# First layer of a graph network: row norms in two chains of four blocks, weight sums held behind the scaled rows, the last four blocks turned together

## The chip, the cores and the metric

The kernel runs on one core of a Trainium2 chip. The metric is the device time of one execution in microseconds (us); the median of several runs is given. In the traces PE is TensorE (matrix products), PEld its loads of stationary operands, DVE is VectorE, ACT ScalarE, POOL GpSimd, and SP the engine that issues most of the transfers.

## The reference

The input x has 1024 rows of 512 values (float32). Rows are normalised and clipped at zero, normalised by column, and passed through a graph convolution with 16384 edges and a loop at each node. Four layers of attention and a gated feed-forward part follow, then a second graph convolution, and x is added. In short:

```python
h = jnp.maximum(_layernorm(x), 0.0); x_in = h
h = gcn((h - mu) * rsqrt(var + EPS) * bn_w + bn_b, src, dst, gcn_in_w, gcn_in_b)
for i in range(4):
    a = attn(ln(h, ln2_w[i], ln2_b[i]), cond, Wq[i], Wk[i], Wv[i], Wo[i])  # 16 groups of 64 rows, 8 heads of 64
    h = h + a
    u = ln(h, ln3_w[i], ln3_b[i]) @ geglu_w[i] + geglu_b[i]
    val, gate = jnp.split(u, 2, axis=-1)
    h = h + (val * gelu(gate)) @ ffo_w[i] + ffo_b[i]
h = gcn(h, src, dst, gcn_out_w, gcn_out_b)
return x + h + x_in
```

Each group attends to 256 condition rows: `cond` has 16 x 256 x 512 values. The kernel treats two groups, 128 rows, as one block; there are eight blocks.

## The kernel before

Rows are held as eight blocks of 128 partitions, `h[0]` to `h[7]`, slices of one tile `hall`. Products are float32. Large products are split in two by two halves and done with seven half products instead of eight (Strassen's scheme in Winograd's form); `sums_of_a` and `sums_of_b` make the sums of halves that this needs, mostly on GpSimd, in four operations for each operand: `weight_sums` for a weight, `sum_cond` for a condition block, `sum_first` for the turned rows of one pair of blocks (`nb` and `nb + 4`).

`seven` does the seven half products for the keys and the values. It holds three banks of PSUM, `b`, `c`, `d` (and `a`). Product 5 goes to `b`, 6 to `c`, 4 to `d`; VectorE makes `u2` from `b` (L713), `u3` from `c` (L716) and writes `c22` from `d` (L718). Then product 3 starts anew in `c` and product 2 in `d`, and VectorE writes `c21` (L723) and `c12` (L725). In the trace both `u2` and `u3` are called `u_k` or `u_v`, and the banks `pb_k`, `pc_k`, `pd_k` or `pb_v` and so on. Products 0 and 1 of the keys of blocks 0 and 1 and of the values of block 0 are done early (`begin`).

The stretch that the change touches lies between the first graph convolution and the queries of the first layer. `aggregate` multiplies the edge counts with the rows, block by block, 16 matmuls a block (blocks 0 and 1 together), and calls `into_h_and_norm`: `into_h` (L672) evicts the block into `h[d]`. After blocks 1 and 3, `ready_first` normalises a pair: `moments` takes `bn_stats` and `bn_aggr` of each block (L155, L156), then `rsqrt`, a chain of 11 small operations (L134, L136, and three times L139, L141, L143) on one column for each block, then `scaled` writes the scaled rows `xn` (L164). `turn_first` transposes scaled rows on TensorE (`tr_ln`, four transposes a block) and writes them with weight and bias into `lnT`, half on ScalarE (L690) and half on VectorE (L688). Behind the aggregates stand, on TensorE: the keys of block 0, the turning of blocks 0 to 3, the values of block 0, the turning of blocks 4 and 5, the keys of block 1, the turning of blocks 6 and 7, and the queries (`qa` and on).

The kernel is written with tile pools; a scheduler orders the instructions of each engine by its own estimate of times, and each engine then runs its list in that order. `tc.issue_after(ins)` keeps what is written under it behind an instruction in the order of issue. `waiting_for(ins, engine)` adds a true wait: the instructions of that engine that are written under it wait until `ins` is done.

Of the kernel before, what the change touches and what calls it, by code (L numbers as in the profile page):

```python
# [8 lines left out]
F32 = mybir.dt.float32  # L9
# [5 lines left out]
OP = mybir.AluOpType  # L15
AX = mybir.AxisListType

P = 128
EPS = 1e-5
# [4 lines left out]
def gnn_kernel(  # L24
# [26 lines left out]
    nc = tc.nc  # L51
# [23 lines left out]
    small = ctx.enter_context(tc.tile_pool(name="small", bufs=4))  # L75
# [5 lines left out]
    @contextmanager  # L81
    def waiting_for(ins, engine):

        traced = nc.cur_bb.bb.instructions
        n = len(traced)
        yield
        for i in traced[n:]:
            if i.engine == engine:
                tc.add_manual_dep(i, ins.ins.name, mybir.DependencyInfo(
                    mybir.DependencyClass.Sync, mybir.DependencyReason.DATA))  # L90
# [33 lines left out]
    def rsqrt(var, name, eps=0.0):  # L124


        k = var.shape[1]

        def t(n, dtype=F32):
            return small.tile([P, k], dtype, tag=f"rs_{n}{k}", name=f"{n}_{name}",  # L130
                              bufs=4 if k == 1 else 2)

        v = t("v")
        rsqrt.first = nc.vector.tensor_scalar(v, var, float(eps), None, OP.add)  # L134
        y = t("y")
        nc.vector.tensor_scalar(y.bitcast(I32), v.bitcast(I32), -0.5, RSQRT_SEED, OP.mult, OP.add)  # L136
        for i in range(3):
            a = t("a")
            nc.vector.scalar_tensor_tensor(a, y, -0.5, v, OP.mult, OP.mult)  # L139
            b = t("b")  # L140
            nc.vector.tensor_tensor(b, a, y, OP.mult)  # L141
            y2 = t("y")
            nc.vector.scalar_tensor_tensor(y2, b, 1.5, y, OP.add, OP.mult)  # L143
            y = y2
        return y

    def moments(xts, name, kept=None):

        n = len(xts)
        mv = kept  # L150
        if mv is None:
            mv = small.tile([P, 2 * n], F32, tag=f"mv{n}", name=f"mv_{name}", bufs=2)
        for i, xt in enumerate(xts):
            st = small.tile([P, 6], F32, tag="st", name=f"st_{name}_{i}")
            nc.vector.bn_stats(st, xt)  # L155
            nc.vector.bn_aggr(mv[:, 2 * i:2 * i + 2], st)  # L156
        return mv, rsqrt(mv.rearrange("p (n c) -> p n c", c=2)[:, :, 1], name, EPS)

    def scaled(xts, mv, rstd, name, to=None):

        xns = []
        for i, xt in enumerate(xts):
            xn = to[i] if to else t512(f"xn_{name}_{i}")
            nc.vector.tensor_scalar(xn, xt, mv[:, 2 * i:2 * i + 1], rstd[:, i:i + 1],  # L164
                                    OP.subtract, OP.mult)
            xns.append(xn)
        return xns

# [28 lines left out]
    h = [hall[:, nb, :] for nb in range(NB)]  # L197
# [18 lines left out]
    def halves_of(t):  # L216
        return t.rearrange("p (a b) -> p a b", a=2)
# [21 lines left out]
    def sum_cond(g, t):  # L239

        b = [t[i][:, j, :] for i in range(4) for j in range(2)]
        sums_of_b(nc.gpsimd, b[0], b[2], b[1], b[3], b[4], b[5], b[6])
        unsaved.append((g, t))
# [34 lines left out]
    conds = {}  # L278
# [18 lines left out]
    def blocks_out(t):  # L297

        return [t[d][:, :, b * M:(b + 1) * M] for d in range(2) for b in range(2)]

    def of_k(w, right):
        return lambda i, to, start: multiply(
            to, w[i], right[i], [(c * P, (c + 1) * P, 0, M) for c in range(2)], start)
# [28 lines left out]
    raw_wk = load_w(Wk[0], "wk_0")  # L332
    fetch_cond(1)
    w_in = load_w(gcn_in_w, "w_in")
    raw_wv = load_w(Wv[0], "wv_0")
# [71 lines left out]
    with tc.issue_after(load_pe.ins), tc.issue_after(load_act.ins):  # L407
        turned = [turn_cond(0, (0, 0))]
# [4 lines left out]
    with tc.issue_after(outside_last.ins):  # L413
        mean, root = moments(xb, "x", x_mean.rearrange("p a b -> p (a b)"))
# [217 lines left out]
    root = rsqrt(pdeg[:, :NB], "deg")  # L632
# [59 lines left out]
    def weight_sums(w, name):  # L692

        s = slots_of(2, name)
        blk = blocks_of_w(w)
        s1, s2, s4 = (halves_of(s[i // 2][:, i % 2, :]) for i in range(3))
        sums_of_a(nc.gpsimd, *blk, s1, s2, s4)
        return [blk[0], blk[1], s4, blk[3], s1, s2, blk[2]]

    def seven(name, product, c11, c12, c21, c22, s1=None):  # L700

        b, c, d = (bank(f"{n}_{name}") for n in ("pb", "pc", "pd"))
        begun = s1 is not None
        if not begun:
            a = bank(f"pa_{name}")
            product(0, a, True)
            s1 = acc_tile(f"s1_{name}")
            nc.scalar.copy(s1, a)  # L710
        product(5, b, True)
        u2 = acc_tile(f"u2_{name}")
        nc.vector.tensor_tensor(u2, b, s1, OP.add)  # L713
        product(6, c, True)
        u3 = acc_tile(f"u3_{name}")
        nc.vector.tensor_tensor(u3, c, u2, OP.add)  # L716
        product(4, d, True)
        nc.vector.tensor_tensor(c22, halves_of(d), halves_of(u3), OP.add)  # L718
        if not begun:
            product(1, a, False)  # L720
            nc.scalar.copy(c11, halves_of(a))
        product(3, c, False)
        nc.vector.tensor_tensor(c21, halves_of(c), halves_of(u2), OP.add)  # L723
        product(2, d, False)
        return nc.vector.tensor_tensor(c12, halves_of(d), halves_of(u2), OP.add)  # L725

    def keys(l, g, wk, begun=None):
        kT, s1 = begun or (slots_of(2, f"kT_{l}_{g}"), None)
        return kT, seven(f"k_{l}_{g}", of_k(wk, conds[l, g]), *blocks_out(kT), s1)

    def values(l, g, wv, begun=None):
        v, s1 = begun or (slots_of(2, f"v_{l}_{g}"), None)
        v11, v21, v12, v22 = blocks_out(v)
        seven(f"v_{l}_{g}", of_v(wv, conds.pop((l, g))), v11, v12, v21, v22, s1)
        return v
# [267 lines left out]
    def sum_first(t, nb):  # L1003

        c0 = nb % 4 * P
        of = [lnT[i][k][:, :, c0:c0 + P] for k in range(2) for i in range(2)]
        sums_of_b(t, *of, *(x[:, :, c0:c0 + P] for x in lnS))

    xns = {}

    def into_h_and_norm(d, pa):
        into_h(d, pa)
        if d in (1, 3):
            ready_first(0, [d - 1, d])

    def ready_first(l, blocks):
        for i in range(0, len(blocks), 2):
            pair = blocks[i:i + 2]
            xns.update({nb: h[nb] for nb in pair} if l == L else norm(pair, f"ln2_{l}_{pair[0]}"))

    def turn_first(l, blocks):

        for nb in blocks:
            xn, c0 = xns.pop(nb), nb % 4 * P
            if l < L:
                turn(xn, lnT[nb // 4], c0, LN2W + l * KC, LN2B + l * KC, f"ln2_{l}_{nb}")
            else:
                pt = transposed(xn, f"hT_{nb}")
                for k in range(2):
                    nc.scalar.copy(lnT[nb // 4][k][:, :, c0:c0 + P],  # L1030
                                   four(pt)[:, 2 * k:2 * k + 2, :])
# [6 lines left out]
    def load_rest(l):  # L1038
        return (load_w(Wq[l], f"wq_{l}"), load_w(Wo[l], f"wo_{l}"),
                load_row(ffo_b, l * D, f"ffb_{l}"))  # L1040
# [13 lines left out]
            nc.gpsimd.dma_start(again[d].bitcast(F32R).rearrange("p a b -> p (a b)"), c_dram[d])  # L1054
        return w, bias

    projections = (weight_sums(raw_wk, "wks_0"), weight_sums(raw_wv, "wvs_0"), *load_rest(0))
    sum_cond(1, turned[1])
    with tc.issue_after(load_w.last.ins):
        for d in range(NB):  # L1060
            nc.sync.dma_start(c_dram[d], C[d].rearrange("p a b -> p (a b)"))
    for l in range(L):

        wk, wv, wq, wo, ffb = projections
        if l:
            wq = weight_sums(wq, f"wqs_{l}")
            lnS = slots_of(3, f"ln2S_{l}")
            sum_first(nc.gpsimd, 0)
            sum_first(nc.gpsimd, 1)
            kv_next = kv(l, 0, wk, wv, lambda: ready_first(l, left_to_turn[2:]))  # L1070
            turn_first(l, left_to_turn)
            next_cond(l, 1)
            sum_first(nc.vector, 2)
            sum_first(nc.vector, 3)
        else:
            lnS = slots_of(3, f"ln2S_{l}")
            kT, last_key = keys(0, 0, wk, begun["k0"])
            with tc.issue_after(last_key.ins):
                ready_first(0, [4, 5])
                turn_first(0, [0, 1, 2, 3])  # L1080
                kv_next = kT, values(0, 0, wv, begun["v0"])
                ready_first(0, [6, 7])
            turn_first(0, [4, 5])
            wq = weight_sums(wq, "wqs_0")
            sum_first(nc.gpsimd, 0)
            sum_first(nc.gpsimd, 1)
            kT_1, _ = keys(0, 1, wk, begun["k1"])
            turn_first(0, [6, 7])
            sum_first(nc.vector, 2)
            sum_first(nc.vector, 3)  # L1090
        qT = queries(l, wq)

        ln3T = [slots_of(2, f"ln3T_{l}_{i}") for i in range(2)]
# [188 lines left out]
```

## Time and profile before

| | |
|---|---|
| median of 3 runs | 2551.42 us (2549.64 to 2553.30) |
| profiled execution | 2551.04 us, of which the profile's span is 2549.3 us |
| mean granted clock of TensorE | 0.999 |
| TensorE busy | 2520.1 us (99%) |
| VectorE busy | 1398.5 us (55%) |
| ScalarE busy, GpSimd busy | 550.9 us, 554.5 us (22% each) |
| from the first key product to the first query product | 119.89 to 156.36 us |

Busy time counts instructions that run; matmuls follow each other in a pipeline, so the end of one is modelled and lies past the start of the next. "Idle before" is the time in which an engine had nothing running, and the name behind the arrow is what it waited for. The granted clock is a share of full speed. Times in timelines count from the start of the span.

### The profile page before, as it was taken

The page shows a single profiled execution, that of the slowest core. Times are in us where ns is not written, and L with a number is a line of the kernel's source. Part 1 is how long each engine was busy: PE and PEld are TensorE (multiplying, and loading weights), DVE is VectorE, ACT ScalarE, POOL GpSimd, SP SyncE. Part 2 cuts the span into 40 slices and gives each one's busy share as a digit, 9 for nine tenths or more (in the row PEclk, how much of TensorE's full clock was granted, in tenths as well). Part 3 has the DMA queues.
Part 4 walks back from the last instruction along what each step waited for, and adds up shares of the span by engine and source line. Part 5 has one row for each costly group of instructions (what it writes and reads, how often), then busy time and mean ns, then how long its engine had stood idle before and what let it go on. Part 6 is the DMA issues. An engine that isn't in the chain of part 4 may idle for free. (4 is left out here: it accounts for less than half of the span.)

```text
span 2549.3 us, 31825 instructions
## 1 busy us (share of the span) xinstructions
PE 2520.1 (99%) x12320; PEld 1744.8 (68%) x12320; DVE 1398.5 (55%) x3060; ACT 550.9 (22%) x1294; POOL 554.5 (22%) x423
## 2 busy tenths in 40 slices
PE   8999999999999999999999999999999999999999
PEld 5668886665578887555587888556676888566565
DVE  9765555544564555644475555644474555554561
ACT  7322222111122222111122222211112222211111
POOL 0401123422300002333310002233310002331410
PEclk9999999999999999999999999999999999999999
DMA  6402223110211111110212211110111112111020
GB/s 177 150 9 92 91 74 121 33 50 12 84 49 67 59 55 58 55 49 17 80 44 75 71 55 58 54 47 20 58 66 59 58 59 67 54 33 62 13 87 34
DMA packets 67133, 156.77 MB, mean 61 GB/s; under 512 B 5576, under 2 KB 5904, under 8 KB 66976
## 3 DMA queue, kind: packets, MB, share of 16 engines
q1 hardware_dynamic: 64880, 149.25, 17.8%
q0 software_dynamic: 1376, 4.30, 0.5%
q8 instruction: 101, 1.65, 0.3%
q10 hardware_dynamic: 720, 1.11, 0.1%
q14 instruction: 56, 0.46, 0.1%
HBM read 133.66 MB, written 20.97 MB: 61 GB/s over the span
## 5 line engine op out<-in xcount | busy, mean ns | idle before, releaser
L293 PE MATMUL ga<-ln3T,wval 128*128 128x512 f32 x512 | 233.9, 593 | 0.0
L1101 POOL TENSOR_TENSOR hall<-hall,ffb 128x512 f32<-128x512 f32 x28 | 35.6, 1271 | 782.4 <-DVE xn_ln L164 782.4
L867 ACT ACTIVATE g<-g,gcols 128x512 f32<-128x512 f32 x128 | 92.3, 721 | 431.8 <-DVE g L880 367.2
L293 PEld LDWEIGHTS ga<-ln3T,wval 128*128 128x128 f32 x512 | 96.0, 190 | 109.9 <-issue 109.1
L765 ACT ACTIVATE pr<-sc,nmax 128x256 f32<-128x256 f32 x256 | 118.2, 474 | 170.7 <-DVE nmax L760 170.5
L941 POOL TENSOR_TENSOR hall<-fu,hall 128x512 f32<-128x512 f32 x24 | 30.5, 1270 | 467.9 <-DVE fu L940 467.9
L293 PE MATMUL pc_k<-ct,wk 128*128 128x256 f32 x512 | 122.7, 383 | 5.0 <-DVE u_k L716 5.0
L293 PE MATMUL fa<-wff,fT 128*128 128x256 f32 x512 | 121.6, 379 | 0.0
L293 PE MATMUL gc<-ln3S,wgate 128*128 128x512 f32 x256 | 120.4, 592 | 1.1 <-DVE gu L877 1.1
L293 PE MATMUL pa_v<-wv,ct 128*128 128x256 f32 x512 | 121.1, 379 | 0.0
L293 PE MATMUL pd_k<-ct,wks 128*128 128x256 f32 x512 | 121.0, 379 | 0.0
L293 PE MATMUL pc_v<-wv,ct 128*128 128x256 f32 x512 | 121.0, 379 | 0.0
L293 PE MATMUL pd_v<-wvs,ct 128*128 128x256 f32 x512 | 120.9, 379 | 0.0
L293 PE MATMUL gb<-ln3S,ges 128*128 128x512 f32 x256 | 120.6, 593 | 0.0
L293 PE MATMUL gd<-ln3T,ges 128*128 128x512 f32 x256 | 120.5, 593 | 0.0
L293 PE MATMUL gd<-ln3S,ges 128*128 128x512 f32 x256 | 120.3, 592 | 0.0
L293 PE MATMUL gc<-ln3T,wgate 128*128 128x512 f32 x256 | 120.3, 592 | 0.0
L816 PE MATMUL pw<-wo,oT 128*128 128x512 f32 x256 | 118.0, 604 | 0.0
L293 PE MATMUL pa_k<-ct,wk 128*128 128x256 f32 x480 | 113.7, 380 | 0.0
L293 PEld LDWEIGHTS fa<-wff,fT 128*128 128x128 f32 x512 | 97.3, 190 | 21.8 <-issue 9.6
L293 PEld LDWEIGHTS pc_k<-ct,wk 128*128 128x128 f32 x512 | 98.2, 192 | 19.3 <-issue 2.9
L293 PEld LDWEIGHTS pa_k<-ct,wk 128*128 128x128 f32 x480 | 90.7, 190 | 23.5 <-issue 11.9
(288 smaller groups left out, 4719.8 us busy)
## 6 DMA issues: line engine op xcount, KB each, us to landing
ct<-cond_dram SPq DMA_DIRECT2D x72, 512.0 KB, 4.4
wval<-in_L_gnn_geglu_w_dram SPq DMA_DIRECT2D x32, 512.0 KB, 4.4
wgate<-in_L_gnn_geglu_w_dram SPq DMA_DIRECT2D x32, 512.0 KB, 4.6
wff<-in_L_gnn_ffo_w_dram SPq DMA_DIRECT2D x32, 512.0 KB, 4.3
cond_dram<-ct SPq DMA_DIRECT2D x24, 512.0 KB, 3.6
cond<-in_L_gnn_cond_dram SPq DMA_DIRECT2D x32, 256.0 KB, 4.6
ct<-cond_dram SPq DMA_DIRECT2D x24, 256.0 KB, 4.4
wk<-in_L_gnn_Wk_dram SPq DMA_DIRECT2D x8, 512.0 KB, 5.5
```

The lines of the kernel that those rows point to most:

```text
L293: nc.tensor.matmul(at, left[:, k, l0:l1], right[:, k, r0:r1], start=start and n == 0 and k == 0, stop=n == len(cols_of) - 1 and k == 1, sk ...
L765: nc.scalar.activation(pr3[:, a, :], ps3[:, a, :], AF.Exp, bias=nmax[:, a:a + 1], accum_out=tot[:, a:a + 1])
L816: nc.tensor.matmul(pw, oT[:, c * P:(c + 1) * P], wo[c // 2][:, c % 2, :], start=(c == 0), stop=(c == HP - 1))
L867: nc.scalar.activation(pre, pre, AF.Gelu, bias=gcols[:, cg:cg + 1])
L941: t.tensor_tensor(h21, halves_of(u2), h21, OP.add)
L1101: t.tensor_tensor(h[nb], h[nb], ffb, OP.add)
```

## The change

The norms of the first layer's first half are no longer taken pair by pair. Each block's moments are taken when the block is evicted, into one of two tiles `mv_first` of four blocks each. After block 3 one `rsqrt` chain on four columns serves blocks 0 to 3, and their four rows are scaled. The second chain, for blocks 4 to 7, is issued behind `c22` of the first keys (`beside` in `seven`), and their rows are scaled behind the last operation of these keys. On GpSimd the sums of the first layer's `Wv` and of condition 1 wait until the first four rows are scaled, and the sums of `Wq` until the last four are. Blocks 4 to 7 are turned together, ahead of the keys of block 1, and VectorE's sums of turned blocks are issued behind these keys.

```diff
@@ -144,25 +144,33 @@
             y = y2
         return y
 
-    def moments(xts, name, kept=None):
-
-        n = len(xts)
-        mv = kept
-        if mv is None:
-            mv = small.tile([P, 2 * n], F32, tag=f"mv{n}", name=f"mv_{name}", bufs=2)
+    def moments_into(mv, xts, name):
+
         for i, xt in enumerate(xts):
             st = small.tile([P, 6], F32, tag="st", name=f"st_{name}_{i}")
             nc.vector.bn_stats(st, xt)
             nc.vector.bn_aggr(mv[:, 2 * i:2 * i + 2], st)
-        return mv, rsqrt(mv.rearrange("p (n c) -> p n c", c=2)[:, :, 1], name, EPS)
+
+    def deviations(mv, name):
+
+        return rsqrt(mv.rearrange("p (n c) -> p n c", c=2)[:, :, 1], name, EPS)
+
+    def moments(xts, name, kept=None):
+
+        mv = kept
+        if mv is None:
+            n = len(xts)
+            mv = small.tile([P, 2 * n], F32, tag=f"mv{n}", name=f"mv_{name}", bufs=2)
+        moments_into(mv, xts, name)
+        return mv, deviations(mv, name)
 
     def scaled(xts, mv, rstd, name, to=None):
 
         xns = []
         for i, xt in enumerate(xts):
             xn = to[i] if to else t512(f"xn_{name}_{i}")
-            nc.vector.tensor_scalar(xn, xt, mv[:, 2 * i:2 * i + 1], rstd[:, i:i + 1],
-                                    OP.subtract, OP.mult)
+            scaled.last = nc.vector.tensor_scalar(xn, xt, mv[:, 2 * i:2 * i + 1],
+                                                  rstd[:, i:i + 1], OP.subtract, OP.mult)
             xns.append(xn)
         return xns
 
@@ -697,7 +705,7 @@
         sums_of_a(nc.gpsimd, *blk, s1, s2, s4)
         return [blk[0], blk[1], s4, blk[3], s1, s2, blk[2]]
 
-    def seven(name, product, c11, c12, c21, c22, s1=None):
+    def seven(name, product, c11, c12, c21, c22, s1=None, beside=lambda ins: None):
 
 
 
@@ -715,7 +723,7 @@
         u3 = acc_tile(f"u3_{name}")
         nc.vector.tensor_tensor(u3, c, u2, OP.add)
         product(4, d, True)
-        nc.vector.tensor_tensor(c22, halves_of(d), halves_of(u3), OP.add)
+        beside(nc.vector.tensor_tensor(c22, halves_of(d), halves_of(u3), OP.add))
         if not begun:
             product(1, a, False)
             nc.scalar.copy(c11, halves_of(a))
@@ -724,9 +732,9 @@
         product(2, d, False)
         return nc.vector.tensor_tensor(c12, halves_of(d), halves_of(u2), OP.add)
 
-    def keys(l, g, wk, begun=None):
+    def keys(l, g, wk, begun=None, *beside):
         kT, s1 = begun or (slots_of(2, f"kT_{l}_{g}"), None)
-        return kT, seven(f"k_{l}_{g}", of_k(wk, conds[l, g]), *blocks_out(kT), s1)
+        return kT, seven(f"k_{l}_{g}", of_k(wk, conds[l, g]), *blocks_out(kT), s1, *beside)
 
     def values(l, g, wv, begun=None):
         v, s1 = begun or (slots_of(2, f"v_{l}_{g}"), None)
@@ -1008,10 +1016,21 @@
 
     xns = {}
 
+    mv_first = [small.tile([P, 2 * 4], F32, tag="mv_first", name=f"mv_first_{i}", bufs=2)
+                for i in range(2)]
+
     def into_h_and_norm(d, pa):
         into_h(d, pa)
-        if d in (1, 3):
-            ready_first(0, [d - 1, d])
+        moments_into(mv_first[d // 4][:, d % 4 * 2:d % 4 * 2 + 2], [h[d]], f"ln2_0_{d}")
+        if d == 3:
+            scale_first(0, deviations(mv_first[0], "ln2_0_0"))
+
+    def scale_first(half, root):
+
+        blocks = range(4 * half, 4 * half + 4)
+        xns.update(zip(blocks, scaled([h[nb] for nb in blocks], mv_first[half], root,
+                                      f"ln2_0_{4 * half}")))
+        scale_first.last = scaled.last
 
     def ready_first(l, blocks):
         for i in range(0, len(blocks), 2):
@@ -1054,8 +1073,10 @@
             nc.gpsimd.dma_start(again[d].bitcast(F32R).rearrange("p a b -> p (a b)"), c_dram[d])
         return w, bias
 
-    projections = (weight_sums(raw_wk, "wks_0"), weight_sums(raw_wv, "wvs_0"), *load_rest(0))
-    sum_cond(1, turned[1])
+    wks_0 = weight_sums(raw_wk, "wks_0")
+    with waiting_for(scale_first.last, mybir.EngineType.Pool):
+        projections = (wks_0, weight_sums(raw_wv, "wvs_0"), *load_rest(0))
+        sum_cond(1, turned[1])
     with tc.issue_after(load_w.last.ins):
         for d in range(NB):
             nc.sync.dma_start(c_dram[d], C[d].rearrange("p a b -> p (a b)"))
@@ -1074,20 +1095,26 @@
             sum_first(nc.vector, 3)
         else:
             lnS = slots_of(3, f"ln2S_{l}")
-            kT, last_key = keys(0, 0, wk, begun["k0"])
+            roots = []
+
+            def root_beside(ins):
+                with tc.issue_after(ins.ins):
+                    roots.append(deviations(mv_first[1], "ln2_0_4"))
+
+            kT, last_key = keys(0, 0, wk, begun["k0"], root_beside)
             with tc.issue_after(last_key.ins):
-                ready_first(0, [4, 5])
-                turn_first(0, [0, 1, 2, 3])
-                kv_next = kT, values(0, 0, wv, begun["v0"])
-                ready_first(0, [6, 7])
-            turn_first(0, [4, 5])
-            wq = weight_sums(wq, "wqs_0")
+                scale_first(1, *roots)
+            turn_first(0, [0, 1, 2, 3])
+            with waiting_for(scale_first.last, mybir.EngineType.Pool):
+                wq = weight_sums(wq, "wqs_0")
+            kv_next = kT, values(0, 0, wv, begun["v0"])
+            turn_first(0, [4, 5, 6, 7])
             sum_first(nc.gpsimd, 0)
             sum_first(nc.gpsimd, 1)
-            kT_1, _ = keys(0, 1, wk, begun["k1"])
-            turn_first(0, [6, 7])
-            sum_first(nc.vector, 2)
-            sum_first(nc.vector, 3)
+            kT_1, last_key = keys(0, 1, wk, begun["k1"])
+            with tc.issue_after(last_key.ins):
+                sum_first(nc.vector, 2)
+                sum_first(nc.vector, 3)
         qT = queries(l, wq)
 
         ln3T = [slots_of(2, f"ln3T_{l}_{i}") for i in range(2)]
```

## The prediction

> **What bounds the kernel now.** I read the page's busy table first, then the waits of TensorE, then TensorE's timeline around the two longest of them, then VectorE's and GpSimd's timelines in the same stretch.
>
> ```profile
> PE 2520.1 (99%) x12320; PEld 1744.8 (68%) x12320; DVE 1398.5 (55%) x3060; ACT 550.9 (22%) x1294; POOL 554.5 (22%) x423
> ```
>
> TensorE is busy 2520.1 of 2549.3 us, so a change that adds no matmul can win only TensorE's gaps (29.2 us in all) or time in which its clock is low.
>
> ```profile
> engine line waited for: us in total, times, longest us
> PE pc_k L293 <- DVE u_k L716: 5.0, 2, 2.5
> ```
>
> The largest entry is two waits of 2.5 us for one line: the fourth product of `seven` in the first layer's keys starts over in the bank `c`, which VectorE must first have read (`u3`, L716). Nearly all other entries lie ahead of the stretch that is changed. TensorE's timeline shows both places (columns: start, duration, instructions, idle time before and its releaser):
>
> ```profile
> 119.89 1.89 PE L293 MATMUL pb_k<-ct,wks 128*128 128x256 f32 x8
> ...
> 123.34 1.89 PE L293 MATMUL pd_k<-ct,wks 128*128 128x256 f32 x8
> 127.72 1.99 PE L293 MATMUL pc_k<-ct,wk 128*128 128x256 f32 x8 [2.50 <-DVE u_k L716]
> ...
> 131.28 1.91 PE L176 MATMUL tr_ln<-ident,xn_ln 128*128 128x128 f32 x16
> ...
> 138.21 1.89 PE L293 MATMUL pc_v<-wv,ct 128*128 128x256 f32 x8
> ...
> 150.41 3.51 PE L293 MATMUL pc_k<-ct,wk 128*128 128x256 f32 x8 [2.53 <-DVE u_k L716]
> 153.76 1.89 PE L293 MATMUL pd_k<-ct,wks 128*128 128x256 f32 x8
> ```
>
> Undisturbed products start 1.73 us apart. After the second wait the same eight matmuls take 3.35 us from start to start. The table by stage says why: its column PEclk (third from the end) is 0.50 there.
>
> ```profile
> 150.14:153.55 3.41, 3.14 (x8) 2.54 (x9) 0.82 (x2) 0.00 (x0) 0.00 (x0) 0.50 0.00 0
> ```
>
> VectorE is late because its small operations between SBUF tiles end together with GpSimd's. Here are GpSimd's timeline and VectorE's:
>
> ```profile
> 101.37 1.30 POOL L211 TENSOR_TENSOR wks<-wk,wk 128x512 f32<-128x512 f32 x1
> 102.75 1.30 POOL L212 TENSOR_TENSOR wk<-wk 128x512 f32<-128x512 f32 x1
> ```
>
> ```profile
> 102.05 0.64 DVE L134 TENSOR_SCALAR v_ln<-mv_ln 128x2 f32<-128x2 f32 x1
> ...
> 102.93 1.14 DVE L139 SCALAR_TENSOR_TENSOR a_ln<-y_ln,v_ln 128x2 f32<-128x2 f32 x1
> ...
> 112.00 2.92 DVE L164 TENSOR_SCALAR xn_ln<-hall,mv_ln,y_ln 128x512 f32<-128x512 f32 x2
> ...
> 126.98 0.69 DVE L716 TENSOR_TENSOR u_k<-pc_k,u_k 128x512 f32<-128x512 f32 x1
> ```
>
> L134 ends at 102.69, GpSimd's L211 at 102.67; L139 at 104.07, L212 at 104.05. An operation of 0.16 us thus costs up to 1.2, and a scaled row 1.46 instead of 0.55 (L164 at 210.87, GpSimd idle). The Trainium skill (SBUF — State Buffer, "Who interferes with whom") calls these ports an exclusive lock, held for a whole instruction; the four ends above agree. Operations that read PSUM, and the moments (L155, L156), keep their 0.7, 0.68 and 0.17 us beside GpSimd.
>
> **What the stretch costs today.** From the first product of the keys (119.89) to the queries (156.36) are 36.47 us. The work in it is 15 products at 1.727 (25.9) and 32 transposes (3.5), 29.4 us. So 7.07 us are lost: 2.66 and 0.11 at the first wait (start to start, and a slow refill), 2.69 and 1.62 at the second, of which 1.62 is the half clock.
>
> **The change, part by part.** The instruction order of the changed program moves nothing on ScalarE but one pair and adds no matmul; VectorE's four chains of 11 small operations become two.
>
> *First half.* The aggregates of blocks 0 to 7 are ready at 99.19, 99.6, 103.0, 106.4, 109.9, 113.3, 116.7 and 120.1 (16 matmuls, 3.41 us, apart). VectorE now evicts (0.70) and takes moments (0.60 and 0.20) as each arrives: blocks 0 and 1 until 102.0, block 2 until 104.6, block 3 until 108.05. GpSimd's first sums end at 106.69 and its next now wait, so the chain of 11 runs free: L134 to L143 of `deg` took 2.26 us for 11 (85.67 to 87.93). It ends near 110.3. Block 4's eviction follows (110.9), then four scaled rows at 0.47 each: 112.8.
>
> *GpSimd held.* Its 4 sums of `wv` and 4 of condition 1 (1.32 each: four took 5.27 from 106.64 to 111.91) run from 112.9 to 118.2 and 123.5. Queued behind them on GpSimd are only the sums of `wq` and of the turned blocks. The products of the values need `wvs` at 130.3, the second keys need condition 1 at 140.7: 12 and 17 us spare, no cost. Beside them VectorE has only evictions and moments, which do not slow. SP's three saves of condition 1 move behind four fetches, the third of which waits for a transposed row (near 129 now); nothing before 185 reads what they bring or free. Cost nothing.
>
> *Keys 0.* Block 7 is evicted at 120.1 and its moments end at 121.7; the first `u_k` waits only for TensorE, 121.8, the second runs 123.5 to 124.2. TensorE wants bank `c` at 119.89 + 3 x 1.727 = 125.07. Spare 0.8 us: the first wait goes, 2.77 us.
>
> *The chain beside the keys.* Seven operations after `c22` (125.25 + 0.61 to 127.2), then L723 (127.1 to 127.7), four more (128.5), L725 (128.7 to 129.3), four scaled rows (131.2). GpSimd idles from 123.5 to 131.2, so none is slowed. What is late next is the values: VectorE turns blocks 0 to 3 (7 x 0.32, in step with ScalarE's 0.44) from 131.2 to 133.7, then `u_v` twice with one turn between, and ends near 135.3; TensorE wants bank `c` at 128.53 + 6.93 = 135.46 (138.21 minus 131.28 today). Spare 0.1 us (today 0.4: L716 there ends at 137.80); I charge 0.1.
>
> *Blocks 4 to 7 turned together.* The same 16 transposes, moved ahead of keys 1; their rows are ready 8 us before. Seven turns in step with ScalarE end about 4.2 us after the transposes start; the second `u_k` there needs to end by 6.9 and ends near 6.1. The second wait goes, 2.69, and with it the half clock, 1.62.
>
> *Sums of the turned blocks* on VectorE come after the last key (149.5 to 152.8), on GpSimd near 141.4 to 147.5; the queries use them 17.2 us after the transposes start, at 156.1. Spare 3 us.
>
> Sum: 2.77 + 2.69 + 1.62 - 0.1 = 7.0 us. The profiled execution took 2551.04 us (its span 2549.3 and 1.7 around it), so 2544.0; it lies 0.38 below the median of the three runs, 2551.42, so the median becomes 2544.4, 0.27% less. About 0.2%, 5.1 us, is what a measurement here can tell from no change: 2546.3.
>
> **Rivals.**
>
> *The half clock is not the gap's.* The granted clock is 0.50 only in stretches of 3.41 us, and the first gap of 2.50 us had none: between 126.25 and 129.66, a whole number of such stretches earlier, TensorE was busy 57%; between 146.73 and 150.14, ahead of the slow one, 34%. If the slow stretch came by chance and is in few of the timed runs, or comes back elsewhere, only 2.77 + 2.69 = 5.4 us are won: 2546.0. For it: the three runs lie 1.8 us apart, about one such stretch. Against it: from 35 us to the end it occurs once, right after the longest idle of that time. The Trainium skill (TensorE: Matmul & The Clock Gate, "Why this matters for your kernels") warns only of gaps beyond some 3 us, by which this gap would not do it; the row of 0.50 behind 2.53 us says otherwise, and the page's free-running window of 3413 ns agrees with the 3.41. Chance 0.12.
>
> *The values wait instead.* If turns and scaled rows take 0.1 us more each than I took, bank `c` of the values comes 1 to 2.5 us late. For it: the spare is the thinnest of all. Against: every duration in it is from uncontended rows. 2545.4 to 2546.9, or 2548.5 with a slow stretch behind it. Chance 0.10.
>
> *Slower: GpSimd's held work meets the second chain.* If the first scaled rows end late, the 10.6 us of sums slide under the chain at 125.9 to 131.2. The two chains of today took 5.9 and some 8.3 us instead of 2.3, four scaled rows would take 5.8 instead of 1.9: 7.5 to 10 us more ahead of the values, less the 7.07 won, and in so long a pause one or two stretches of half clock at 1.6: 2553.4 to 2557.4. It begins when the scaled rows end after 115.3 and is whole only near 120, against my 112.8. For it: one queue holds all of VectorE's work. Against: 2.4 us of margin. Chance 0.07.
>
> *It does not do what it says.* An order of instructions is not a time: if VectorE's evictions still lag as today, one or both waits stay, 2548 to 2551.5. Chance 0.04.
>
> **Numbers.** The forecast 2544.4 has 0.67. Faster by over 0.2%: that case, half of the first rival and half of the second, 0.78; within 0.2%: the other halves and the last, 0.15; slower: the third, 0.07. The range runs from 2542.4 (the spread of the runs, 1.9, below) to 2548.0: it leaves out the slower rival, the last, and the worst of the second.
>
> **What would show it.** Right: no wait of `pc_k` for `u_k`; 29.4 us from the first product of the keys to the queries; the chains 2.3 us long; clock 1.00 from 120 on; GpSimd idle from 106.7 to about 113. Wrong: a wait of `pc_v` for `u_v`; L134 to L143 of the second chain above 0.2 us each; GpSimd still busy after 126; or a slow stretch of 3.41 us elsewhere after 35 us.

## The result, and the profile after

The median falls from 2552.15 us (2549.64 to 2553.30, eight runs) to 2543.72 us (2543.31 to 2544.29, eight runs). The ratio of the times is 0.9968, with a 95% interval of 0.9957 to 0.9978. Measured again beside the last experiments, the same two kernels took 2551.35 and 2543.39 us, ratio 0.9969 [0.9957, 0.9981]. The profiled execution took 2543.89 us, its span 2542.1, where that of before took 2551.04 and 2549.3.

The busy table of the changed kernel:

```profile
PE 2517.7 (99%) x12320; PEld 1744.3 (69%) x12320; DVE 1382.8 (54%) x3038; ACT 550.1 (22%) x1294; POOL 553.6 (22%) x423
```

TensorE has the same 12320 matmuls and is busy 2.4 us less. Of these 2.05 lie between the first key product and the queries (31.45 us busy before, 29.40 now), most of them what the half clock had stretched. VectorE has 22 instructions fewer, two chains of 11. Among the waits of TensorE in the changed kernel (what waited for what: us in total, times, longest) the largest, apart from two of 3.7 us in the first 11 us, are now these:

```profile
PE pa_kT L301 <- DVE v_deg L134: 2.4, 1, 2.4
PE fd L301 <- DVE fs L921: 1.9, 1, 1.9
```

Neither lies in the stretch that was changed, and no wait of `pc_k` for `u_k` or of `pc_v` for `u_v` is left (5.0 us before). TensorE's timeline of the changed kernel shows the same (start, duration, instructions; an idle time would stand at the end of a line):

```profile
119.67 1.89 PE L301 MATMUL pb_k<-ct,wks 128*128 128x256 f32 x8
...
124.85 1.89 PE L301 MATMUL pc_k<-ct,wk 128*128 128x256 f32 x8
...
135.24 1.89 PE L301 MATMUL pc_v<-wv,ct 128*128 128x256 f32 x8
...
145.62 1.89 PE L301 MATMUL pc_k<-ct,wk 128*128 128x256 f32 x8
...
149.07 1.45 PE L301 MATMUL qa<-ln2T,wq 128*128 128x512 f32 x3
```

From the first product of the keys to the queries are 149.07 - 119.67 = 29.40 us, 36.47 before. The table by stage has TensorE busy all of it (the length and TensorE's busy time are both 29.40), at a granted clock of 1.00 (third from the end):

```profile
119.67:149.07 29.40, 29.40 (x153) 26.20 (x152) 19.91 (x48) 6.59 (x16) 14.07 (x15) 1.00 0.24 87
```

VectorE's and GpSimd's timelines of the changed kernel show why:

```profile
108.00 0.17 DVE L134 TENSOR_SCALAR v_ln<-mv_first 128x4 f32<-128x4 f32 x1
...
109.99 0.16 DVE L143 SCALAR_TENSOR_TENSOR y_ln<-b_ln,y_ln 128x4 f32<-128x4 f32 x1
...
110.73 1.91 DVE L172 TENSOR_SCALAR xn_ln<-hall,mv_first,y_ln 128x512 f32<-128x512 f32 x4
...
123.33 0.69 DVE L724 TENSOR_TENSOR u_k<-pc_k,u_k 128x512 f32<-128x512 f32 x1 [0.96 <-PE pc_k L301]
...
134.15 0.68 DVE L724 TENSOR_TENSOR u_v<-pc_v,u_v 128x512 f32<-128x512 f32 x1
```

```profile
105.14 1.28 POOL L222 TENSOR_TENSOR wks<-wk,wks 128x512 f32<-128x512 f32 x1
112.72 1.29 POOL L219 TENSOR_TENSOR wvs<-wv,wv 128x512 f32<-128x512 f32 x1 [6.29 <-DVE xn_ln L172]
...
131.16 1.27 POOL L219 TENSOR_TENSOR wqs<-wq,wq 128x512 f32<-128x512 f32 x1 [7.98 <-DVE xn_ln L172]
```

GpSimd waits 6.29 us for the first four scaled rows and 7.98 us for the last four. In these gaps VectorE's chain runs in 108.00 to 110.15 us, no small operation takes over 0.17, and a scaled row takes 1.91 / 4 = 0.48 us. So the first `u3` (L724) waits 0.96 us for TensorE and runs at 123.33; in the profile before it ran at 126.98.

### The profile page after: what moved, and what is told of

Same layout as the page of the kernel before. It is cut to its first block, busy times and chain, and to the rows that moved or that the text cites. A ratio compares the mean times of both kernels' runs of the same rounds, so it can differ in the third digit from the quotient of the medians.

```text
span 2542.1 us, 31802 instructions
## 1 busy us (share of the span) xinstructions
PE 2517.7 (99%) x12320; PEld 1744.3 (69%) x12320; DVE 1382.8 (54%) x3038; ACT 550.1 (22%) x1294; POOL 553.6 (22%) x423
## 5 line engine op out<-in xcount | busy, mean ns | idle before, releaser
L301 PEld LDWEIGHTS pc_v<-wv,ct 128*128 128x128 f32 x512 | 97.3, 190 | 13.2
```

The costliest lines, as they stand in the source:

```text
L301: nc.tensor.matmul(at, left[:, k, l0:l1], right[:, k, r0:r1], start=start and n == 0 and k == 0, stop=n == len(cols_of) - 1 and k == 1, sk ...
```

## The experiments

All are edits of the kernel after, unless said otherwise; all times are medians, and ratios are to the kernel before on the same chip. The theory: both waits of TensorE came from GpSimd's sums that lay on VectorE's short operations between SBUF tiles, so the two holds are the whole gain. Rival: the rest of the change (chains of four blocks, the last four turned together) brings some of it by itself. A second question was how the half clock comes about, and so how much of the gain a profile can show.

**Both holds taken off, everything else kept.** Every engine keeps its order of instructions; only GpSimd no longer waits.

```diff
-    with waiting_for(scale_first.last, mybir.EngineType.Pool):
-        projections = (wks_0, weight_sums(raw_wv, "wvs_0"), *load_rest(0))
-        sum_cond(1, turned[1])
+    projections = (wks_0, weight_sums(raw_wv, "wvs_0"), *load_rest(0))
+    sum_cond(1, turned[1])
...
-            with waiting_for(scale_first.last, mybir.EngineType.Pool):
-                wq = weight_sums(wq, "wqs_0")
+            wq = weight_sums(wq, "wqs_0")
```

> The changed kernel without both holds on GpSimd; every engine's order stays as in the changed kernel. Theory (GpSimd's sums lengthen VectorE's small operations, and the holds take them out of the way): the first chain runs beside the sums of wv from 108.0 and takes some 8 us instead of 2.2, four scaled rows 4 to 6 instead of 1.9, block 7 is evicted near 126, the second u_k ends near 128.4 where bank c is wanted at 124.85: a wait of 3 to 3.6 us comes back in the first keys, and in most runs a slow stretch of the clock for 1.6; 2547 to 2549. Rival (fewer small operations and the new order do it, the holds nothing): 2543.7, no wait.

Measured: 2551.19 us, ratio 1.0002 [0.9993, 1.0011]: all of the gain is gone. VectorE's timeline without the holds:

```profile
109.11 1.20 DVE L136 TENSOR_SCALAR y_ln<-v_ln 128x4 int32<-128x4 int32 x1
...
117.69 4.84 DVE L172 TENSOR_SCALAR xn_ln<-hall,mv_first,y_ln 128x512 f32<-128x512 f32 x4
...
128.81 0.69 DVE L724 TENSOR_TENSOR u_k<-pc_k,u_k 128x512 f32<-128x512 f32 x1
```

and TensorE's:

```profile
129.56 3.78 PE L301 MATMUL pc_k<-ct,wk 128*128 128x256 f32 x8 [4.54 <-DVE u_k L724]
133.13 2.38 PE L301 MATMUL pd_k<-ct,wks 128*128 128x256 f32 x8
```

GpSimd's sums run beside the chain, and the ends coincide again: L136 above ends at 110.31, this sum at 110.29.

```profile
109.01 1.28 POOL L221 TENSOR_TENSOR wvs<-wvs,wv 128x512 f32<-128x512 f32 x1
```

The one chain of four blocks now takes 108.00 to 117.1, 9.1 us instead of 2.15, and the four scaled rows 4.84 instead of 1.91. The delay shows at one product, for which TensorE waits 4.54 us, and the clock is at half for two stretches behind it (3.57 and 2.21 us from start to start instead of 1.73). The place was as expected; the wait and the time were larger than I expected. The chain of four blocks without a hold is no better than the pairs of before.

**The second hold alone taken off**, so that GpSimd's sums of `Wq` follow those of condition 1 at once. It was run twice, on two chips.

```diff
-            with waiting_for(scale_first.last, mybir.EngineType.Pool):
-                wq = weight_sums(wq, "wqs_0")
+            wq = weight_sums(wq, "wqs_0")
```

> The changed kernel with the sums of wq no longer held; the first hold stays. They then follow the sums of condition 1 and run from 123.2 to 128.5, over the second chain at 125.7. Theory: some 7 of the 11 operations take 0.5 to 0.7 instead of 0.2, the last scaled row ends near 133 instead of 131, and the values' bank c, with 0.4 us of spare, waits 1.5 us: 2545.2. This is a small part of the slower rival of the prediction, whose full price was 7.5 to 10 us. Rival (the second chain is hidden beside the keys): 2543.7.

Measured: 2546.21 us (2544.34 to 2547.53), ratio 0.9982 [0.9973, 0.9991]. The second chain, 124.94 to 129.47, has two operations of 1.14 and 1.12 us beside GpSimd's sums at 122.42 to 127.61, and the values wait in its place:

```profile
135.77 1.99 PE L301 MATMUL pc_v<-wv,ct 128*128 128x256 f32 x8 [1.08 <-DVE u_v L724]
```

From the first key product to the queries are 30.75 us, 1.35 more than with the hold. So the second hold is worth this wait, and more in most runs: the median is 1.0 us above the 2545.2 that was expected. The repeat asked where the more comes from:

> The changed kernel with the second hold off, run again for the cause of the spread of its times. The pause at the values is 1.1 us in each. Theory (a stretch of half clock of 3.4 us follows a pause of this length in some runs and not in others): two groups of times some 1.6 us apart, the lower at 2544.8 to 2545.2 us; a profile from the upper group shows the granted clock at half right behind 135 us. Rival (the spread comes from elsewhere in the run): no stretch of half clock between 119 and 153 us, and a spread as wide as that of the changed kernel beside it.

Measured: 2545.97 us (2544.21 to 2547.00), ratio 0.9978 [0.9969, 0.9987], the wait 1.09 us. Both profiled executions came from the low end of the times and have no half clock in the stretch, so the place of the excess was not seen. Its runs spread over 2.8 us, those of the changed kernel beside it over 1.1, so the excess goes with the hold that is missing.

**The first hold alone, in the order of before.** An edit of the kernel before: no chain of four, no other order of turning.

```diff
-            nc.vector.tensor_scalar(xn, xt, mv[:, 2 * i:2 * i + 1], rstd[:, i:i + 1],
-                                    OP.subtract, OP.mult)
+            scaled.last = nc.vector.tensor_scalar(xn, xt, mv[:, 2 * i:2 * i + 1],
+                                                  rstd[:, i:i + 1], OP.subtract, OP.mult)
...
-    projections = (weight_sums(raw_wk, "wks_0"), weight_sums(raw_wv, "wvs_0"), *load_rest(0))
-    sum_cond(1, turned[1])
+    wks_0 = weight_sums(raw_wk, "wks_0")
+    with waiting_for(scaled.last, mybir.EngineType.Pool):
+        projections = (wks_0, weight_sums(raw_wv, "wvs_0"), *load_rest(0))
+        sum_cond(1, turned[1])
```

> The kernel before with the first hold alone: the sums of wv and of condition 1 wait for the scaled rows of blocks 2 and 3; every engine's order stays as before. Theory: the first wait of the keys goes (2.8 us), since the second chain runs free and blocks 4 to 7 are evicted in time; the second stays, as its chain still meets the sums of turned blocks; about 2549.4, one wait of 2.5 left. Rival (the order and the shorter chains are needed): no change, 2552.2.

Measured: 2546.17 us (2545.36 to 2549.30), ratio 0.9985 [0.9976, 0.9994]. The first wait is gone and the second is there, 2.53 us, as expected; the time is 3.2 us below my figure. About 0.8 of this is the kernel before, 2551.33 on this chip where I had taken 2552.2. Most of the rest is half clock that I had kept in the figure, 1.62 us in the profile of before; this profiled execution has none.

```profile
146.69 1.96 PE L293 MATMUL pc_k<-ct,wk 128*128 128x256 f32 x8 [2.53 <-DVE u_k L716]
```

What makes the second wait is seen in VectorE's and GpSimd's timelines of this kernel:

```profile
143.77 0.65 DVE L143 SCALAR_TENSOR_TENSOR y_ln<-b_ln,y_ln 128x2 f32<-128x2 f32 x1
144.46 1.49 DVE L164 TENSOR_SCALAR xn_ln<-hall,mv_ln,y_ln 128x512 f32<-128x512 f32 x2
```

```profile
143.66 0.74 POOL L206 TENSOR_TENSOR ln2S<-ln2T,ln2S 128x256 f32<-128x256 f32 x1
```

GpSimd's sums of the turned blocks run at 139.56 to 145.2, 0.72 to 0.75 us each, and the chain of blocks 6 and 7 steps at their pace. If that is all, holding these sums must do for the second wait what the first hold does for the first.

**Two holds in the order of before.** The kernel before with the hold above and this one; the order of instructions of TensorE, VectorE, ScalarE and GpSimd is that of before.

```diff
             wq = weight_sums(wq, "wqs_0")
-            sum_first(nc.gpsimd, 0)
-            sum_first(nc.gpsimd, 1)
+            with waiting_for(scaled.last, mybir.EngineType.Pool):
+                sum_first(nc.gpsimd, 0)
+                sum_first(nc.gpsimd, 1)
```

> The order of the kernel before on every engine, with the first hold and, new here, GpSimd's sums of the first two pairs of turned blocks held behind the scaled rows of blocks 6 and 7. Theory (the waits of TensorE come only from GpSimd's sums lying on VectorE's short chains): the chain of blocks 6 and 7 runs free, its small operations take under 0.2 us each, the pause of 2.5 us at the fourth key product goes as the first did, the stretch from the first key product to the queries is 29.4 us, and the time is 2543.7 to 2544.5 us, as that of the changed kernel. Rival (the order of the blocks is needed too: halving the chains and turning the last four together give something by themselves): a pause of 1 us or more stays in the stretch, and the time is 2545.5 us or more.

Measured: 2543.82 us (2542.93 to 2546.73), ratio 0.9971 [0.9960, 0.9983]; the changed kernel beside it 2543.39. VectorE's timeline of this kernel:

```profile
142.59 0.16 DVE L143 SCALAR_TENSOR_TENSOR y_ln<-b_ln,y_ln 128x2 f32<-128x2 f32 x1
142.79 1.00 DVE L164 TENSOR_SCALAR xn_ln<-hall,mv_ln,y_ln 128x512 f32<-128x512 f32 x2
143.71 0.69 DVE L716 TENSOR_TENSOR u_k<-pc_k,u_k 128x512 f32<-128x512 f32 x1
```

The last small operation takes 0.16 instead of 0.65 us, the two rows 1.00 instead of 1.49, and from the first key product to the queries are 148.94 - 119.50 = 29.44 us, with TensorE busy in all of them:

```profile
119.50:148.94 29.44, 29.44 (x154) 26.07 (x152) 21.20 (x62) 5.48 (x13) 15.55 (x17) 1.00 0.26 92
```

The theory holds here: four chains of two blocks in the old order, with GpSimd held twice, do what the change does. The new order is one way to get both chains out of GpSimd's way, and is not needed for it.

**The other two parts, undone one at a time.** First the chains of four blocks, made again as chains of two (the same `rsqrt` on half of the columns, twice), with both holds kept:

```diff
-            scale_first(0, deviations(mv_first[0], "ln2_0_0"))
+            scale_first(0, pair_roots(0))
...
+    def pair_roots(half):
+        return [deviations(mv_first[half][:, 4 * i:4 * i + 4], f"ln2_0_{4 * half + 2 * i}")
+                for i in range(2)]
...
-                    roots.append(deviations(mv_first[1], "ln2_0_4"))
+                    roots.extend(pair_roots(1))
```

> The changed kernel with chains on two columns: two chains of 11 for each half instead of one, 22 small operations more, everything else as in the changed kernel (the scheduler moves three transposes of block 4 ahead by two products). Theory: with GpSimd held a small operation costs 0.2 us, 4.4 in all, and both places have room: 2543.7 to 2544.5. Rival (the number of small operations is what counts): 4.4 us more or a part of it in front of the values, 2546 to 2548.

Measured: 2544.35 us (2542.88 to 2545.24), ratio 0.9970 [0.9959, 0.9982]; the stretch is 29.50 us. Then blocks 6 and 7 turned behind the keys of block 1 again:

```diff
-            turn_first(0, [4, 5, 6, 7])
+            turn_first(0, [4, 5])
...
             kT_1, last_key = keys(0, 1, wk, begun["k1"])
-            with tc.issue_after(last_key.ins):
-                sum_first(nc.vector, 2)
-                sum_first(nc.vector, 3)
+            turn_first(0, [6, 7])
+            sum_first(nc.vector, 2)
+            sum_first(nc.vector, 3)
```

> The changed kernel with blocks 6 and 7 turned behind the second keys again and VectorE's sums of turned blocks behind them. Theory: the second wait went because the chain of blocks 6 and 7 is no longer ahead of the second keys, not because of the turning; 2543.7, within 0.5. Rival (turning the four together is what removes the second wait): 2546.4 without a slow stretch, 2548 with it.

Measured: 2544.19 us (2542.88 to 2545.72), ratio 0.9975 [0.9966, 0.9984]; the stretch is 29.40 us without a wait. Neither part moves the time by more than the runs spread (2.4 and 2.8 us).

**A pause of a chosen length.** What does a pause of TensorE cost here, and when does the half clock follow it? Copies of a tile onto itself on ScalarE, ahead of the `u3` of block 1's keys, make the fourth product of these keys wait; the queries of the first layer are held in TensorE's order behind the keys. With 4, 6 and 8 copies (the line with `range` is the only difference):

```diff
         nc.vector.tensor_tensor(u2, b, s1, OP.add)
+        if name == "k_0_1":
+            for _ in range(6):
+                nc.scalar.copy(u2, u2)
...
-        nc.vector.tensor_tensor(c21, halves_of(c), halves_of(u2), OP.add)
+        seven.c21 = nc.vector.tensor_tensor(c21, halves_of(c), halves_of(u2), OP.add)
...
-        qT = queries(l, wq)
+        with waiting_for(seven.c21, mybir.EngineType.PE) if not l else nullcontext():
+            qT = queries(l, wq)
```

Four copies:

> The changed kernel with four copies of u2 onto itself on ScalarE in the second keys, which delays u3 and with it bank c; the output is the same. Pause of TensorE about 1.1 us (0.65 for each copy, less 1.5 of room). Theory (a slow stretch follows a stretch of 3.41 us in which TensorE idled for more than about half): the pause leaves at least 68% of any such stretch busy, so no slow stretch: 2544.8, runs within 1 us. Rival (slow stretches come on their own): the same.

Measured: 2545.86 us (2544.61 to 2546.78), ratio 0.9978 [0.9968, 0.9987]; the pause is 0.91 us and the clock 1.00 behind it, as expected, but the time is 1.1 us above the expected 2544.8. The one stretch of half clock in this profile is far off, at 2384.8. Six copies:

> As the one with four copies, with six: a pause of about 2.4 us, as the waits of the kernel before. Theory: in some runs a slow stretch follows, in others not, by where the 3.41 us fall: 2546.1 in some runs and 2547.7 in others, so runs spread over 1.6 us. Rival (slow stretches come on their own): 2546.1 in all runs, within 1 us, and clock 1.00 behind the pause.

Measured: 2547.93 us, ratio 0.9983 [0.9974, 0.9992], in two groups: 2545.26 to 2546.08 (five runs) and 2547.93 to 2549.19 (six). The pause is 2.21 us; the profiled execution, of the lower group, has full clock behind it. Two groups were expected, but 1.6 us apart; their medians, 2545.5 and 2548.4, are 2.9 us apart. Eight copies:

> As the one with four copies, with eight: a pause of about 3.7 us. Theory: a slow stretch follows in nearly all runs: 2549 (3.7 and 1.6 more than the changed kernel). Rival (slow stretches come on their own): 2547.4.

Measured: 2548.24 us (2547.30 to 2551.12), ratio 0.9990 [0.9981, 0.9999]; the pause is 3.51 us, and the next eight matmuls take 3.36 us from start to start instead of 1.73. The table by stage, at the edges of the stretch of half clock:

```profile
144.78:148.20 3.42, 0.16 (x1) 0.00 (x0) 0.59 (x1) 2.67 (x5) 0.46 (x1) 1.00 0.00 0
148.20:151.61 3.41, 3.16 (x8) 2.57 (x9) 0.80 (x2) 0.00 (x0) 0.00 (x0) 0.50 0.00 0
```

Four copies once more:

> The changed kernel with four extra copies ahead of the sums of the fourth key block, run again: a pause of 0.9 us at the fourth key product. If a pause costs its own length alone, 2544.6 us; if a stretch of half clock follows it in most runs, 2546.2 us. The profile shows which it was in that run: the granted clock between 146 and 153 us. A slow stretch near the end of the run, at the pauses of the last layer, would put the excess there and not at the pause that was made.

Measured: 2546.22 us (2544.93 to 2547.55), ratio 0.9980 [0.9971, 0.9989]. The profiled execution took 2544.95; it has the pause of 0.91 us, full clock between 146 and 153, and one stretch of half clock at 27.35. The median is that of the second guess, but the stretch of half clock was not seen at the pause.

**The changed kernel again**, on the chip of the two holds in the old order:

> The changed kernel itself, to have its time on the same chip as its neighbours of this call: 2543.7 us, within 1 us, no pause in the stretch from the first key product to the queries, which is 29.4 us long.

Measured: 2543.39 us (2543.02 to 2544.15, six runs); the stretch is 148.36 - 118.97 = 29.39 us, without a wait.

**What a pause costs.** Every run has its mean granted clock, to three places. One whole stretch of half clock takes 0.5 x 3.41 / 2545 = 0.00067 off it, so a run at 1.000 has had no whole one. These runs by themselves (median, number of runs), beside what the stretch from the first key product to the queries loses in a profile, against 29.40 us and without the half clock:

| kernel | lost, by the profile | median at clock 1.000 | above the changed kernel | median of all |
|---|---|---|---|---|
| changed (both measurements) | 0 | 2543.31 (7 of 14) | | 2543.72, 2543.39 |
| second hold off (two chips) | 1.35 | 2544.48 (6 of 22) | 1.2 | 2546.21, 2545.97 |
| six copies | 2.45 | 2545.51 (5 of 11) | 2.2 | 2547.93 |
| before with the first hold | 2.76 | 2545.95 (6 of 11) | 2.6 | 2546.17 |
| before (three chips) | 2.66 + 0.11 + 2.69 = 5.46 | 2548.61 (10 of 86) | 5.3 | 2551.33, 2551.51, 2551.35 |

With the clock at full speed a pause costs what the stretch loses by it, within 0.25 us. What the medians show beyond that goes with a lower clock: for before, 2551.35 - 2548.61 = 2.7 us.

**When the half clock follows.** In the profile of before the two stretches start at 27.25 and 150.13 us, 122.88 us apart, 36 times 3.413; without the holds they start at 86.32 and 127.28, 12 times 3.413 apart. So the stretches stand on a grid that runs on through the whole execution, and the profiles of like kernels have it in different places. I cut all 14 profiles of this study on their own grids, from 20 us to the end (their records of the clock begin at 13.5 to 16.2 us). Of the windows at full clock in which TensorE was busy 45% or less there are 12, and 10 of them were followed by a window of half clock; of 94 windows between 46% and 80%, none was. The two exceptions are busy 43% and 44%, so the border is not sharp. One of them holds the pause of the profile with six copies:

```profile
145.39:148.80 3.41, 1.49 (x7) 1.37 (x8) 1.38 (x2) 1.02 (x2) 0.01 (x1) 1.00 0.00 0
148.80:152.21 3.41, 3.41 (x15) 2.43 (x14) 1.86 (x4) 0.00 (x0) 0.00 (x0) 1.00 0.00 0
```

The kernel before with the first hold has a pause of 2.53 us that falls on a grid line, and stays at full clock (its table by stage):

```profile
142.06:145.47 3.41, 2.10 (x10) 1.52 (x8) 3.27 (x7) 0.00 (x0) 3.07 (x5) 1.00 0.00 0
145.47:148.88 3.41, 2.19 (x10) 1.98 (x11) 1.95 (x5) 0.00 (x0) 0.00 (x0) 1.00 0.00 0
```

TensorE is busy 62% and 64% of the two windows, neither under 45%. The second pause of before, as long, left 1.16 us of one window (34%) and cost the half clock:

```profile
146.72:150.13 3.41, 1.16 (x6) 0.68 (x4) 3.31 (x6) 0.00 (x0) 2.13 (x4) 1.00 0.00 0
```

An estimate from the border of 45%: 1.88 us of idle (55% of 3.413) must fall into one window. A pause of 2.53 us does so in (3.41 + 2.53 - 3.76) / 3.41 = 0.64 of the places of the grid, one of 2.21 us in 0.55, one of 3.51 us in 0.93, and one of 1.1 us in none. That goes with six of eleven runs in the upper group at 2.21 us and all eleven below clock 1.000 at 3.51 us. But the clock of a run does not say where it was low, and the two groups at 2.21 us are 2.9 us apart, more than the 1.62 us of one stretch in the profile of before. No profile of the upper group was taken, so what its runs have besides is not shown.

The Trainium skill (TensorE: Matmul & The Clock Gate, "Why this matters for your kernels") warns of gaps beyond some 3 us. By that, neither of the two pauses of before would have cost the half clock; the profile of before has it behind 2.53 us, so the measurement decides, and a pause inside one window need not be that long. The same page ("What's actually happening") says that the window of 3413 ns runs free of the kernel's start, and the grid of these profiles agrees.

Open: by this estimate pauses of 0.9 and 1.1 us are too short to bring half clock of their own, yet 16 of 22 runs with the second hold off and all 22 with four copies were below 1.000, most of them 1.4 to 3.3 us above what the pause costs, while no run of the changed kernel was above 2544.29. The two stretches that were seen in these profiles lie elsewhere (27.35 and 2384.76 us, behind waits that all these kernels have). Such stretches also stand in profiles without any pause from the first key product to the queries: at 27.18 (last four blocks turned in pairs), 85.94 (two holds in the old order) and 2384.35 us (chains of pairs). The wait near 2381 us lies at the border in itself: the window around it was busy 1.52 and 1.53 us of 3.41 in the two profiles with a stretch behind it, 1.55 and 1.56 in two of those without. So a small shift of the work against the grid could decide there. Whether it does in the kernels with a short pause, and why no run of the changed kernel has it, was not settled.

## Why the prediction was right, and where its sizes were off

*The first wait and the second.* The prediction had both go, 2.77 and 2.69 us. They did, and the work between the first key product and the queries is 29.40 us, as it was added up from 15 products and 32 transposes.

*The steps.* The first chain ended at 110.15 (forecast 110.3), the scaled rows at 112.64 (112.8), GpSimd's held sums began at 112.72 (112.9) and ended at 123.18 (123.5), the first `u3` ended at 124.02 (124.2), the second chain at 128.26 (128.5) and the last scaled rows at 131.03 (131.2). The first key product itself came 0.22 us earlier than before, about what separates these pairs; so the intervals were right to 0.1 us. That the holds do it, and not the shorter work, was argued there only through the chain's price; the kernels without holds and with holds in the old order show it. They show that VectorE's small operations are short when GpSimd's do not run beside them; what in the chip makes the two end together was not tested.

*The charge at the values.* This term was mis-sized. I had VectorE end its second `u_v` at 135.3, 0.1 us ahead of TensorE, and charged 0.1. It ended at 134.83 against 135.24: 0.41 us to spare, no charge. The seven turns took 2.36 us on VectorE (130.94 to 133.3), not the 2.5 in step with ScalarE that I gave them. The rival that lived on this spare, the values waiting, did not come; it came with the second hold off, at 1.08 us, where the prediction had 1 to 2.5 for it.

*The half clock.* In the profiled execution the term of 1.62 us was right: 7.07 us went from the stretch, 0.22 ahead of it, and the rest of the run is the same within 0.2, so the profiled times differ by 2551.04 - 2543.89 = 7.15, forecast 7.0. For the median it was too small. The medians differ by 8.4 us (eight runs each) and 7.96 (measured again): 5.3 for the pauses and 2.7 to 3.1 for half clock, where the prediction had 1.62. It took the one stretch behind the second pause to be what a median run loses; only 10 of 86 runs of before were at clock 1.000, and 17 were at 0.998 or less, which takes more than two stretches. The forecast of 2544.4 was 0.7 above the measured 2543.72: 0.15 by the difference of the profiled executions, 0.38 because it kept the distance of before's median from its profiled execution, and 0.17 because the median of the changed kernel lies below its own. That it came so near was in part luck: the three runs of before that it started from have a median 0.73 us below that of eight.

*The rival that the half clock is not the gap's* falls. It stands in the window right behind the pause in the profile with 3.51 us, and twice behind the 4.54 us of the kernel without holds. What the prediction set beside it, 57% busy in the window of the first pause and 34% in that of the second, fits the border: one side of 45% and the other.

*The slower rival*, GpSimd's held work under the second chain, did not come: GpSimd was idle from 123.18 to 131.16. That its price was of the right order is seen at the other chain, without holds: 9.1 - 2.15 + 4.84 - 1.91 = 9.9 us, where the prediction had 7.5 to 10. At the second chain only a small part of it was tried: with the second hold off, that chain took 4.53 us instead of 2.60.

## What to carry to other kernels

When an engine's tiny operations take one microsecond in place of 0.16, look for another engine's instructions that end at the same instant; a wait that holds the other engine's work until the short chain is through can be worth more than shortening the chain, if the held work has slack (12 us here). First try the holds alone in the old order: here they gave all of the gain. And price a pause of the matrix engine by many runs: the profile shows its length, but whether the half clock follows goes, by these profiles, with where the pause lies in a window of 3.41 us, and that differs from execution to execution.

## What was not expected of the hardware

Two pauses of the same 2.53 us, at the same product of nearly the same kernel, cost 2.69 + 1.62 us in one execution and 2.76 in the other; the busy share of the window, 34% or 62 and 64%, told them apart. Over 14 profiles the border lay near 45% busy. One kernel with one pause of 2.21 us has two times, 2545.5 us at clock 1.000 and 2548.4 below it; how much of the 2.9 us between them is the half clock right behind the pause was not seen.
